# Four-layer cross-attention on one core: projections on column tiles, transposes on row tiles, four score banks

## The chip, the cores and the metric

The kernel runs on one core of one Trainium2 chip. What is measured is the device time of one execution in microseconds (us). A core has a matrix engine (TensorE, "PE" in the profile, its weight loads "PEld"), VectorE (DVE), ScalarE (ACT), GpSimd (POOL) and SyncE (SP, here only the issuer of transfers). TensorE writes into PSUM, which has eight banks here, each of 128 partitions by 512 f32 columns; other engines copy from there to SBUF.

TensorE's array can work whole (128 rows by 128 columns), or divided into tiles: two row tiles of 64 rows, four of 32, two column tiles of 64 columns, or four of 32. Row tiles take operands that are short in the contracted dimension, column tiles take stationary operands with few columns, and several tiles work side by side. Which of these divisions is set is called a mode here.

## The reference

Sixteen batches of queries `x` (100 x 256) pass through four layers of cross-attention with the same context (361 x 256), all in f32. Cut to what matters:

```python
def attention(q, k, v):                       # 16 heads
    return softmax(q @ k.T * scale) @ v

# L0: heads of 16; layer norm of query and context, biases, then a feed-forward block 256 -> 1024 -> 256
x = x + attention(ln(x) @ wq + bq, ln(ctx) @ wk + bk, ln(ctx) @ wv + bv) @ wo + bo
x = x + gelu(ln(x) @ w1 + b1) @ w2 + b2
# L1: heads of 64; RMS norm of the query, plain context
x = x + attention(rms(x) @ wq, ctx @ wk, ctx @ wv) @ wo
# L2: heads of 64; rotary positions on q and k, a mask, layer norm at the end
x = ln(x + attention(rope(x @ Wq), rope(ctx @ Wk), ctx @ Wv, mask) @ Wo) * gamma + beta
# L3: heads of 16; layer norm of query and context, biases
x = x + attention(ln(x) @ Wq + bq, ln(ctx) @ Wk + bk, ln(ctx) @ Wv + bv) @ Wo + bo
```

## The kernel before, in words

All weights are loaded once into SBUF ("slabs") and stay there. A batch is written as a list of pieces of work; each piece is a function that issues a few instructions of one engine, with the buffers it reads, writes and takes. `Plan.add` records it, `Plan.order` sorts all pieces of all sixteen batches into one fixed order by simulating the engines with costs written into the kernel (`on_pe`, `on_dve`, `on_act`, `on_pool`), and the instructions are then issued in that order. So the order on each engine is fixed when the program is built, and pieces of neighbouring batches stand between each other; `plan.order(2.5e4)` sets by how much an older batch goes first.

The planner knows TensorE's modes. Each piece for TensorE has one, `MODE_SWITCH` is the cost that the planner sets for a change of mode, and `KEEP_MODE` a bias toward staying in the mode. There are five: `full` (whole array), `row64`, `row16` (row tiles of 32 rows), `col64`, `col16` (column tiles of 32 columns). For the planner's own count a piece with no mode is a mode of its own.

Which work runs in which mode before:

- `full`: transposes of the context (`keys_T`, L630), once as it is and once normalized; transposes of the queries (`queries_T`, L595), five per batch; keys projections (`project_T`, L618, 361 columns); values projections (L1025 with 512 columns in the layers with heads of 64, L935 with 256 in the others); output projections (`project_out`, L857, 256 columns).
- `col64`: query projections and the first feed-forward product (`project_narrow`, L610, 100 columns); values products of heads of 64 (`weighted`, L814).
- `col16`: values products of heads of 16 (L814), on four column tiles.
- `row64` and `row16`: scores (L703) of heads of 64 and of heads of 16, which stand in strips of 32 rows.
- `row64`: transposes of the probabilities (`transposed`, L782). The rows 0 to 63 and 64 to 99 go to a row tile and a PSUM bank each.

The attention goes in units of four heads. For a unit TensorE writes four score banks; VectorE takes the maximum of each (L753), ScalarE the exponential with its sum (L756), VectorE the reciprocal of the sums (L728), GpSimd multiplies (L735). TensorE transposes the probabilities, VectorE or ScalarE copies them out as `pT` (L545 or L543), and TensorE multiplies them with the values. The helper `copied` (L543, L545) lets the planner choose between ScalarE and VectorE for each copy.

All products and scores share the eight PSUM banks. A second resource, `ps_sc`, has `SCORE_BANKS` = 5 shares; a score bank holds a share until its exponential is done, so that scores can't fill all of PSUM.

The normalized queries `z` (L579) come from statistics on VectorE (L557) and a power on GpSimd (L567), and `queries_T` transposes them.

Of the kernel before, what the change touches and what calls it, by code (L numbers as in the profile page):

```python
# [17 lines left out]
P = 128  # L18
B, S, E = 16, 100, 256
SK = 361  # L20
H = 16
NKC = 3
KC = (128, 128, SK - 256)
SKP = NKC * P
BIG = 3.0e38
SCORE_BANKS = 5

# [39 lines left out]
class Work:  # L67
    __slots__ = (
        "engines", "fn", "bufs", "takes", "next", "then", "n_after", "ready", "tail", "batch",
        "mode", "index", "start", "end", "engine",  # L70
    )
# [24 lines left out]
class Plan:  # L96

    MODE_SWITCH = {"full": 190, "row64": 170, "row16": 170, "col64": 145, "col16": 145, None: 190}

# [19 lines left out]
    def add(self, engines, fn, reads=(), writes=(), takes=(), mode=None, begun=()):  # L119


        w = Work()
        w.engines, w.fn, w.mode, w.batch = engines, fn, mode, self.batch
        w.index = len(self.work)
# [33 lines left out]
    def order(self, lag):  # L158
# [10 lines left out]
        while left:  # L169
# [3 lines left out]
            for w in ready:  # L173
# [24 lines left out]
                for e, occ, lat in w.engines:  # L198
                    s = max(t, free_at[e])
                    if e == "PE" and w.mode != mode:  # L200
                        lat = lat + self.MODE_SWITCH[w.mode]
                    if cost is None or s + lat < cost - 1:
                        engine, cost, start = e, s + lat, s
                late = start
                if engine == "PE" and w.mode != mode and run < self.RUN:
                    late += self.KEEP_MODE
# [5 lines left out]
            if e == "PE":  # L212
                run = run + occ if w.mode == mode else occ
                if w.mode != mode:
                    occ += self.MODE_SWITCH[w.mode]
                mode = w.mode
            free_at[e] = start + occ
            w.start, w.end, w.engine = start, end, e
            for b in w.takes:
                slots = self.free[b.cls]  # L220
                slots.sort()
                _, i = slots.pop(0)
                b.slot, b.ap = i, self.slots[b.cls][i]
                if b.cls in turn:
                    turn[b.cls] += 1
# [22 lines left out]
def tile_xattn_layers(  # L248
# [18 lines left out]
    def slots_of(name, n, shape, dtype=F32, pool=const):  # L267
# [9 lines left out]
        "ctxr": slots_of("ctxr", 1, [P, NKC, E]),  # L277
        "cT": slots_of("cT", 2, [P, 2, SK]),
        "zT": slots_of("zT", 2, [P, 2, SK]),
        "rot": slots_of("rot", 1, [P, 2, SK]),  # L280
# [308 lines left out]
    def queries_T(src, p, name):  # L589

        t, ps = plan.buf(f"xT{p}", name), plan.buf("ps", f"{name}_ps")

        def fn(_):
            for c in range(2):
                nc.tensor.transpose(  # L595
                    ps.ap[:, c * S : (c + 1) * S], src.ap[:, c * P : (c + 1) * P], ident[:S, :S]
                )

        plan.add(on_pe((S, 2)), fn, reads=[src], writes=[ps], takes=[t], mode="full")
        copied(  # L600
            lambda: t.ap.rearrange("p c s -> p (c s)"), lambda: ps.ap[:, : 2 * S], 2 * S, [ps], [t]
        )
        return t

    def project_narrow(ps, wt, m, rhs, n):

        for c in range(2):
            for t in range(2):
                m0 = m * P + t * 64
                nc.tensor.matmul(  # L610
                    ps[t * 64 : (t + 1) * 64, :n], lhsT=wt[:, c, m0 : m0 + 64], rhs=rhs[:, c, :n],
                    start=(c == 0), stop=(c == 1), tile_position=(0, t * 64),
                )

    def project_T(ps, wt, m, rhs, n):

        for c in range(2):
            nc.tensor.matmul(  # L618
                ps[:, :n], lhsT=wt[:, c, m * P : (m + 1) * P], rhs=rhs[:, c, :n],
                start=(c == 0), stop=(c == 1),  # L620
            )

    def keys_T(ct, cls, b):
        t = plan.buf(cls, f"{cls}_{b}")
        for c in range(2):
            ps = plan.buf("ps", f"{cls}_ps_{b}_{c}")

            def fn(_, c=c, ps=ps):
                for j, n in enumerate(KC):
                    nc.tensor.transpose(  # L630
                        ps.ap[:, j * P : j * P + n], ct.ap[:n, j, c * P : (c + 1) * P],
                        ident[:n, :n],
                    )

            plan.add(on_pe((P, 3)), fn, reads=[ct], writes=[ps], takes=[t], mode="full")
            copied(
                lambda c=c: t.ap[:, c, :], lambda ps=ps: ps.ap[:, :SK], SK, [ps], [t]
            )
        return t
# [31 lines left out]
    class Attention:  # L671
# [17 lines left out]
        def unit(self, i):  # L689
# [9 lines left out]
            def scores(_):  # L699
# [11 lines left out]
                on_pe((half, 4 * len(groups))), scores, reads=[self.q, *keys],  # L711
                writes=[*banks.values(), *shares.values()], mode=f"row{hd}",
            )
# [84 lines left out]
        def weighted(self, i, groups, pTs):  # L798
# [4 lines left out]
            def fn(_):  # L803
# [19 lines left out]
                writes=[ps],  # L823
                mode=f"col{hd}",
            )
# [24 lines left out]
    def project_out(oT, nch, wname, resid, p, name):  # L850

        ps, t = plan.buf("ps", f"{name}_ps"), plan.buf(f"x{p}", name)
        wt = w[wname]

        def fn(_):
            for c in range(nch):
                nc.tensor.matmul(  # L857
                    ps.ap[:S, :E], lhsT=oT.ap[:, c, :], rhs=wt[:, c, :], start=(c == 0),
                    stop=(c == nch - 1),
                )  # L860

        def add(_):
            nc.vector.tensor_tensor(t.ap, ps.ap[:S, :E], resid.ap, ALU.add)

        plan.add(
            on_pe((E, 2 * nch)), fn, reads=[oT, slab_of[wname]], writes=[ps], takes=[t], mode="full"
        )
        plan.add(on_dve(E), add, reads=[ps, resid], writes=[t])
        return t


    def small_heads_layer(L, b, xt, zT, names, fq, fk):
# [5 lines left out]
        def keys(m):  # L878
            ps = plan.buf("ps", f"L{L}_k_ps_{b}_{m}")

            def fn(_):
                project_T(ps.ap, w[wk], m, zT.ap, SK)

            def biased(eng):
# [9 lines left out]
            plan.add(  # L894
                on_pe((SK, 4)), fn, reads=[zT, weight(wk)], writes=[ps], takes=[kb[m]], mode="full"
            )
# [14 lines left out]

        def queries(_, ps=ps):
            for m in range(2):
                project_narrow(ps.ap[:, m * S :], w[wq], m, qn.ap, S)

        plan.add(
            on_pe((S, 8)), queries, reads=[qn, weight(wq)], writes=[ps], takes=[qT], mode="col64"
        )
# [11 lines left out]
        for j, n in enumerate(KC):  # L930
            ps = plan.buf("ps", f"L{L}_v_ps_{b}_{j}")

            def values(_, j=j, n=n, ps=ps):
                for c in range(2):
                    nc.tensor.matmul(  # L935
                        ps.ap[:n, :E], lhsT=zT.ap[:, c, j * P : j * P + n], rhs=w[wv][:, c, :],
                        start=(c == 0), stop=(c == 1),
                    )

            plan.add(  # L940
                on_pe((E, 4)), values, reads=[zT, weight(wv)], writes=[ps], takes=[v], mode="full"
            )
# [26 lines left out]
    def large_heads_layer(L, b, xt, xT, cT, names, rot, cap):  # L969
# [4 lines left out]
        for u in range(2):  # L974
            ps = plan.buf("ps", f"L{L}_q_ps_{b}_{u}")

            def queries(_, u=u, ps=ps):
                for m in range(4):
                    project_narrow(ps.ap[:, m * S :], w[wq], 4 * u + m, xT.ap, S)

            def dst(a, u=u):
# [3 lines left out]
                on_pe((S, 16)), queries, reads=[xT, weight(wq)], writes=[ps], takes=[qT],  # L985
                mode="col64",
            )
# [11 lines left out]
        def keys(m):  # L999
            ps, kt = plan.buf("ps", f"L{L}_k_ps_{b}_{m}"), plan.buf(f"kT{p}", f"L{L}_k_{b}_{m}")  # L1000
            kb[m] = kt

            def fn(_):
                project_T(ps.ap, w[wk], m, cT.ap, SK)

            plan.add(
                on_pe((SK, 4)), fn, reads=[cT, weight(wk), *([rot] if rot else [])], writes=[ps],
                takes=[kt], mode="full",
            )
# [8 lines left out]
        def values(half):  # L1018
            v = vb[half] = plan.buf(f"v{p}", f"L{L}_v_{b}_{half}")
            for j, n in enumerate(KC):  # L1020
                ps = plan.buf("ps", f"L{L}_v_ps_{b}_{half}_{j}")

                def fn(_, j=j, n=n, ps=ps):
                    for c in range(2):
                        nc.tensor.matmul(  # L1025
                            ps.ap[:n, :], lhsT=cT.ap[:, c, j * P : j * P + n],
                            rhs=w[wv][:, c, half * 512 : (half + 1) * 512],
                            start=(c == 0), stop=(c == 1),
                        )

                plan.add(
                    on_pe((512, 4)), fn, reads=[cT, weight(wv)], writes=[ps], takes=[v], mode="full"
                )
                copied(
                    lambda j=j, n=n: v.ap[:n, j, :], lambda n=n, ps=ps: ps.ap[:n, :], 512, [ps], [v]
                )
# [20 lines left out]
    def feed_forward(b, xt):  # L1057
# [9 lines left out]

        def hidden(_):
            for f in range(8):
                project_narrow(pss[f // 4].ap[:, f % 4 * S :], w[w1], f, yT.ap, S)  # L1070

        plan.add(
            on_pe((S, 32)), hidden, reads=[yT, weight(w1)], writes=pss, takes=[hT], mode="col64"
        )

# [88 lines left out]
    with tc.manual_schedule():  # L1164
        for work in plan.order(2.5e4):
            if work.fn is not None:
                work.fn(work.engine)

# [48 lines left out]
```

## Time and profile before

| | |
|---|---|
| Runs | 2083.6, 2086.1, 2088.1 us; median 2086.1 |
| The profiled execution | 2088.5 us, of which the profile's span is 2086.4 us |
| Granted TensorE clock, mean | 0.988 |
| TensorE matmul records and instructions of weights | 23,737 each |
| VectorE, ScalarE, GpSimd busy in the span | 68%, 51%, 46% |
| Copies of `pT` on VectorE (L545) | 667, 265.7 us in all |
| Transfers | 27.37 MB, most of it in the first 50 us |

A share of busy time is the time in which at least one instruction of the engine is under way. Matmuls overlap one another, and the ends of their records are modelled, so for TensorE the time from one start to the next says more than a duration. An f32 matmul leaves two records, a transpose one. A row such as `128*64 128x100` is a stationary operand of 128 rows by 64 columns, and a moving operand of 128 rows by 100 columns. Rows of the timeline merge neighbours of one line.

### The profile page before, as it was taken

The page shows a single profiled execution, that of the slowest core. Times are in us where ns is not written, and L with a number is a line of the kernel's source. Part 1 is how long each engine was busy: PE and PEld are TensorE (multiplying, and loading weights), DVE is VectorE, ACT ScalarE, POOL GpSimd, SP SyncE. Part 2 cuts the span into 40 slices and gives each one's busy share as a digit, 9 for nine tenths or more (in the row PEclk, how much of TensorE's full clock was granted, in tenths as well). Part 3 has the DMA queues.
Part 4 walks back from the last instruction along what each step waited for, and adds up shares of the span by engine and source line. Part 5 has one row for each costly group of instructions (what it writes and reads, how often), then busy time and mean ns, then how long its engine had stood idle before and what let it go on. Part 6 is the DMA issues. An engine that isn't in the chain of part 4 may idle for free.

```text
span 2086.4 us, 59681 instructions
## 1 busy us (share of the span) xinstructions
PE 2038.3 (98%) x23737; PEld 1432.2 (69%) x23737; DVE 1409.7 (68%) x4035; ACT 1056.2 (51%) x3190; POOL 955.4 (46%) x1521
## 2 busy tenths in 40 slices
PE   8999999999999999999999999999999999999997
PEld 6667667676776766767676676767667666676765
DVE  4556766767577675776767667676776767767674
ACT  3545445545455454554555555454554545545543
POOL 3244635436254452644526354352544526445362
PEclk9999999999999999999999999999999999999996
DMA  7000000000000000000000000000000000000000
GB/s 282 2 2 12 4 10 4 4 12 4 10 4 4 11 4 12 2 12 4 4 12 4 10 4 4 12 4 10 4 4 12 4 12 4 10 4 4 2 4 3
DMA packets 14430, 27.37 MB, mean 13 GB/s; under 512 B 3346, under 2 KB 12360, under 8 KB 12616
## 3 DMA queue, kind: packets, MB, share of 16 engines
q1 hardware_dynamic: 14152, 23.56, 3.5%
q8 instruction: 187, 3.06, 0.6%
q14 instruction: 91, 0.75, 0.1%
HBM read 21.92 MB, written 1.64 MB: 11 GB/s over the span
## 4 chain that ended last, share of the span: by engine, by line
PE 91%; DVE 5%; ACT 1%; issue 1%; POOL 1%; DMA 1%; SPq 0%; ACTq 0%; DVEq 0%; POOLq 0%
PE ps L618 19%; PE ps L1025 16%; PE ps L703 12%; PE ps L814 11%; PE ps L857 10%; PE ps L782 10%; PE ps L610 6%; PE ps L935 4%; ACT pT L543 1%; PE ps L595 1%; PE ps L630 1%; DVE two L753 1%; DVE mv L557 1%; POOL mv L567 1%; PE ps L441 1%
## 5 line engine op out<-in xcount | busy, mean ns | idle before, releaser
L735 POOL TENSOR_SCALAR prob<-prob,two 100x361 f32<-100x361 f32 x1024 | 569.6, 574 | 559.7 <-DVE two L728 510.6
L756 ACT ACTIVATE prob<-ps,two 100x361 f32<-100x361 f32 x1024 | 564.3, 565 | 128.3 <-DVE two L753 97.4
L753 DVE TENSOR_REDUCE two<-ps 100x1 f32<-100x361 f32 x1024 | 475.9, 523 | 191.9 <-PE ps L703 191.9
L1025 PE MATMUL ps<-slab,cT 128*128 128x512 f32 (+1 forms) x768 | 373.2, 609 | 0.0
L618 PE MATMUL ps<-cT,slab 128*128 128x361 f32 x1024 | 353.7, 483 | 0.5 <-ACT pT L543 0.5
L545 DVE COPY pT<-ps 128x216 f32<-128x216 f32 (+1 forms) x667 | 265.7, 429 | 113.9 <-PE ps L782 103.4
L703 PE MATMUL ps<-kT,qT 32*100 32x181 f32 (+3 forms) x4096 | 303.2, 330 | 0.6 <-DVE qT L923 0.6
L782 PEld LDWEIGHTS ps<-ident,prob 36*128 36x128 f32 (+1 forms) x6144 | 223.7, 140 | 99.4 <-POOL prob L735 41.5
L703 PEld LDWEIGHTS ps<-kT,qT 32*100 32x100 f32 (+1 forms) x4096 | 228.6, 165 | 92.2 <-issue 42.1
L543 ACT COPY pT<-ps 128x384 f32<-128x384 f32 (+1 forms) x357 | 153.1, 461 | 230.1 <-PE ps L782 178.8
L782 PE MATMUL ps<-ident,prob 64*128 64x64 f32 (+1 forms) x6144 | 256.6, 228 | 2.8 <-POOL prob L735 2.0
L618 PEld LDWEIGHTS ps<-cT,slab 128*128 128x128 f32 x1024 | 184.5, 191 | 95.2 <-issue 3.7
L1025 PEld LDWEIGHTS ps<-slab,cT 128*128 128x128 f32 (+1 forms) x768 | 129.3, 183 | 119.8 <-issue 102.4
L756 ACT ACTIVATION_READ_ACCUMULATOR prob<-ps,two 100x1 f32 x1024 | 210.4, 205 | 0.0
L610 PEld LDWEIGHTS ps<-xT,slab 128*64 128x64 f32 x3584 | 157.1, 138 | 41.4 <-ACT prob L756 17.5
L567 POOL TENSOR_TENSOR mv<-mv,neg_half 128x1 f32<-128x1 f32 (+1 forms) x96 | 57.4, 604 | 258.9 <-DVE mv L564 254.4
L610 PE MATMUL ps<-xT,slab 128*64 128x100 f32 x3584 | 172.9, 252 | 0.9 <-ACT xT L543 0.9
L656 POOL TENSOR_TENSOR sw<-sw,rot 128x361 f32<-128x361 f32 x128 | 105.1, 822 | 148.7 <-DVE sw L652 146.2
L543 ACT COPY v<-ps 128x512 f32<-128x512 f32 (+1 forms) x159 | 93.2, 586 | 152.1 <-PE ps L1025 151.1
L814 PE MATMUL ps<-pT,v 128*64 128x100 f32 (+1 forms) x3072 | 152.7, 253 | 5.0 <-ACT pT L543 4.3
L857 PE MATMUL ps<-slab,oT 128*100 128x256 f32 x640 | 152.7, 386 | 0.0
L814 PEld LDWEIGHTS ps<-pT,v 128*64 128x64 f32 (+1 forms) x3072 | 135.9, 137 | 19.2 <-ACT pT L543 6.6
(85 smaller groups left out, 2060.5 us busy)
## 6 DMA issues: line engine op xcount, KB each, us to landing
slab<-slabs_dram SPq DMA_DIRECT2D x12, 1024.0 KB
ctxr<-ctx_dram SPq DMA_DIRECT2D x16, 256.0 KB
ctxr<-ctx_dram SPq DMA_DIRECT2D x16, 105.0 KB
x<-x_dram SPq DMA_DIRECT2D x16, 100.0 KB
out_dram<-x SPq DMA_DIRECT2D x16, 100.0 KB
mask<-mask_dram SPq DMA_DIRECT2D x16, 45.1 KB
rows<-rowvecs_dram SPq DMA_DIRECT2D x1, 640.0 KB
cst<-consts_dram SPq DMA_DIRECT2D x1, 362.0 KB
```

What stands on the lines that cost most here:

```text
L543: nc.scalar.copy(dst(), src())
L545: nc.vector.tensor_copy(dst(), src())
L610: nc.tensor.matmul(ps[t * 64 : (t + 1) * 64, :n], lhsT=wt[:, c, m0 : m0 + 64], rhs=rhs[:, c, :n], start=(c == 0), stop=(c == 1), tile_posi ...
L618: nc.tensor.matmul(ps[:, :n], lhsT=wt[:, c, m * P : (m + 1) * P], rhs=rhs[:, c, :n], start=(c == 0), stop=(c == 1),)
L703: nc.tensor.matmul(banks[h].ap[:S, k0:k1], lhsT=self.q_of(h), rhs=self.k_of(h)[:, k0:k1], start=(k0 == 0), stop=(k1 == SK), skip_group_che ...
L735: nc.gpsimd.tensor_scalar(p.ap[:S, :SK], p.ap[:S, :SK], rsum.ap[:S, j : j + 1], 1.0, ALU.mult, ALU.mult,)
L753: nc.vector.tensor_reduce(neg_max.ap[:S, 0:1], s(), AX.X, ALU.max, negate=True)
L756: nc.scalar.activation(prob.ap[:S, :SK], s(), AF.Exp, bias=neg_max.ap[:S, 0:1], accum_out=sums.ap[:S, j : j + 1],)
L782: nc.tensor.transpose(tp(t)[:, j, c, :], prob.ap[q0:q1, c * P : (c + 1) * P], ident[q0:q1, q0:q1],)
L814: nc.tensor.matmul(ps.ap[t * w0 : (t + 1) * w0, cols], lhsT=lhsT, rhs=pTs[h][0].ap[:n, pTs[h][1], c, :], start=(c == 0), stop=(c == NKC - ...
L857: nc.tensor.matmul(ps.ap[:S, :E], lhsT=oT.ap[:, c, :], rhs=wt[:, c, :], start=(c == 0), stop=(c == nch - 1),)
L1025: nc.tensor.matmul(ps.ap[:n, :], lhsT=cT.ap[:, c, j * P : j * P + n], rhs=w[wv][:, c, half * 512 : (half + 1) * 512], start=(c == 0), stop ...
```

## The change

All work of `full` mode but the one-time set-up of the weights moves to a divided array.

- A new helper `on_columns` splits a product along the columns of its stationary operand, in widths of 64 or 32, one matmul for each column tile. `project_T` uses it and replaces `project_narrow` too; values and output projections call it directly. The last context chunk of 105 rows becomes 64 + 41 or 32 + 32 + 32 + 9, and 100 queries become 64 + 36 or 32 + 32 + 32 + 4.
- Projections take either width: `mode=ANY_COLUMNS`. The planner uses the one that is set, and the first, `col64`, where neither is. The function gets the chosen mode as its argument (`work.fn(work.mode)`).
- `queries_T` and `keys_T` transpose in halves of 64 rows on two row tiles, each into a bank of its own, as `transposed` did before. A query tile is then copied out in two copies of 128 and 72 columns rather than in one of 200. A context tile is one piece of twelve transposes with two banks and three copies of 384, 256 and 82 columns; before, it was two pieces of three transposes, a bank and a copy of 361 columns each. The tiles `cT` and `zT` grow from 361 to 384 columns per half.
- `row16` and `col16` are renamed `row32` and `col32`, which they were in fact; `MODE_SWITCH` has new values.
- `SCORE_BANKS` goes from 5 to 4, and the lag between batches from 2.5e4 to 3e4.

```diff
-SCORE_BANKS = 5
+SCORE_BANKS = 4
...
-    MODE_SWITCH = {"full": 190, "row64": 170, "row16": 170, "col64": 145, "col16": 145, None: 190}
+    MODE_SWITCH = {"row64": 160, "row32": 175, "col64": 145, "col32": 130, None: 190}
...
+        w.modes = mode if isinstance(mode, tuple) else (mode,)
...
-                if engine == "PE" and w.mode != mode and run < self.RUN:
+                if engine == "PE" and mode not in w.modes and run < self.RUN:
                     late += self.KEEP_MODE
...
+                run = run + occ if mode in w.modes else occ
+                if mode not in w.modes:
+                    mode = w.modes[0]
+                    occ += self.MODE_SWITCH[mode]
+                w.mode = mode
...
     def queries_T(src, p, name):
...
+        banks = [plan.buf("ps", f"{name}_ps{i}") for i in range(2)]
+        parts = ((0, 64), (64, S))
...
             for c in range(2):
-                nc.tensor.transpose(
-                    ps.ap[:, c * S : (c + 1) * S], src.ap[:, c * P : (c + 1) * P], ident[:S, :S]
-                )
-
-        plan.add(on_pe((S, 2)), fn, reads=[src], writes=[ps], takes=[t], mode="full")
+                for i, (q0, q1) in enumerate(parts):
+                    nc.tensor.transpose(
+                        tp(i)[:, c, :], src.ap[q0:q1, c * P : (c + 1) * P], ident[q0:q1, q0:q1]
+                    )
+
+        plan.add(
+            on_pe((64, 2), least=55), fn, reads=[src], writes=banks, takes=[t], mode="row64"
+        )
...
+    def on_columns(mode, out_f, lhsT, rhs, start, stop):
+
+        width = int(mode[3:])
+        n = lhsT.shape[1]
+        for t in range(0, n, width):
+            t1 = min(t + width, n)
+            nc.tensor.matmul(
+                out_f(t, t1), lhsT=lhsT[:, t:t1], rhs=rhs, start=start, stop=stop,
+                tile_position=(0, t),
+            )
+
+    def project_T(mode, ps, wt, m, rhs, n):
+
+        for c in range(2):
+            on_columns(
+                mode, lambda t, t1: ps[t:t1, :n], wt[:, c, m * P : (m + 1) * P], rhs[:, c, :n],
+                c == 0, c == 1,
+            )
+
+    ANY_COLUMNS = ("col64", "col32")
+    HALVES = ((0, 64), (64, P))
...
     def keys_T(ct, cls, b):
...
+            for j, n in enumerate(KC):
+                for c in range(2):
+                    for i, (r0, r1) in enumerate(HALVES):
+                        r1 = min(r1, n)
+                        nc.tensor.transpose(
+                            tp(i)[:, c, j, : r1 - r0], ct.ap[r0:r1, j, c * P : (c + 1) * P],
+                            ident[r0:r1, r0:r1],
+                        )
...
+        copied(lambda: dst(0, 0, NKC), lambda: tp(0), 2 * NKC * 64, [banks[0]], [t])
+        copied(lambda: dst(1, 0, 2), lambda: tp(1)[:, :, 0:2, :], 4 * 64, [banks[1]], [t])
         copied(
+            lambda: t.ap[:, :, 2 * P + 64 : SK], lambda: tp(1)[:, :, 2, :last], 2 * last,
+            [banks[1]], [t],
+        )
...
-        def fn(_):
+        def fn(mode):
             for c in range(nch):
-                nc.tensor.matmul(
-                    ps.ap[:S, :E], lhsT=oT.ap[:, c, :], rhs=wt[:, c, :], start=(c == 0),
-                    stop=(c == nch - 1),
+                on_columns(
+                    mode, lambda t0, t1: ps.ap[t0:t1, :E], oT.ap[:, c, :], wt[:, c, :], c == 0,
+                    c == nch - 1,
                 )
...
-            on_pe((E, 2 * nch)), fn, reads=[oT, slab_of[wname]], writes=[ps], takes=[t], mode="full"
+            on_pe((E, 2 * nch)), fn, reads=[oT, slab_of[wname]], writes=[ps], takes=[t],
+            mode=ANY_COLUMNS,
...
-        for work in plan.order(2.5e4):
+        for work in plan.order(3e4):
             if work.fn is not None:
-                work.fn(work.engine)
+                work.fn(work.mode)
```

The keys and values projections and the query projections change in the same way as the output projection shown.

## The prediction

> **What bounds the kernel now.** I read the page's engine totals first, then the chain of waits, then TensorE's waits, then TensorE's timeline inside one batch.
>
> ```profile
> PE 2038.3 (98%) x23737; PEld 1432.2 (69%) x23737; DVE 1409.7 (68%) x4035; ACT 1056.2 (51%) x3190; POOL 955.4 (46%) x1521
> PE   8999999999999999999999999999999999999997
> PE 91%; DVE 5%; ACT 1%; issue 1%; POOL 1%; DMA 1%; SPq 0%; ACTq 0%; DVEq 0%; POOLq 0%
> ```
>
> TensorE is busy 98% of the span and is 91% of the chain that ended last; VectorE, the next, has 677 us idle. So the time is what TensorE has to do, plus the little that it waits. Its waits:
>
> ```profile
> PE ps L595 <- DVE z L579: 18.3, 15, 5.3
> PE ps L814 <- ACT pT L543: 10.5, 47, 0.3
> ```
>
> The columns are total us, times, longest us. All TensorE waits together are 44 us, and these two are most of it: a transpose of normalized queries that waits for VectorE, and the product with the values that waits for its transposed probabilities.
>
> Busy does not mean streaming. In the timeline (start, duration, engine, line, shapes, number of records), the time from one start to the next, where the rows before and after are in another tiling, is the price of a run of matmuls in one tiling:
>
> ```profile
> 1060.23 2.97 PE L610 MATMUL ps<-xT,slab 128*64 128x100 f32 x64
> 1063.13 1.32 PE L782 MATMUL ps<-ident,prob 64*128 64x64 f32 x36
> 1064.39 1.99 PE L935 MATMUL ps<-slab,zT 128*128 128x256 f32 x8
> ...
> 1085.51 0.91 PE L610 MATMUL ps<-xT,slab 128*64 128x100 f32 x16
> 1086.35 1.48 PE L703 MATMUL ps<-kT,qT 64*100 64x181 f32 x16
> ...
> 1094.07 0.58 PE L782 MATMUL ps<-ident,prob 64*128 64x64 f32 x12
> 1094.59 2.70 PE L618 MATMUL ps<-cT,slab 128*128 128x361 f32 x8
> 1097.21 1.48 PE L703 MATMUL ps<-kT,qT 64*100 64x181 f32 x16
> ...
> 1107.39 3.70 PE L857 MATMUL ps<-slab,oT 128*100 128x256 f32 x16
> 1111.02 0.87 PE L703 MATMUL ps<-kT,qT 32*100 32x181 f32 x16
> 1111.82 0.39 PE L595 MATMUL ps<-ident,x 100*128 100x100 f32 x2
> ...
> 1118.10 1.98 PE L1025 MATMUL ps<-slab,cT 128*128 128x512 f32 x4
> 1120.01 1.32 PE L782 MATMUL ps<-ident,prob 64*128 64x64 f32 x36
> ...
> 1123.98 1.24 PE L814 MATMUL ps<-pT,vs 128*32 128x100 f32 x48
> 1125.16 0.58 PE L782 MATMUL ps<-ident,prob 64*128 64x64 f32 x12
> ```
>
> Each f32 matmul leaves two records, a transpose one. Full array: L1025 takes 1120.01 - 1118.10 = 1.91 us for 4 x 512 columns, L857 3.63 us for 16 x 256. The difference, 1.72 us for 2048 columns, is 0.84 ns a column, and 1.91 - 2048 x 0.84 ns leaves 0.19 us that belongs to the run and not to its columns. L618 confirms it: 8 x 361 x 0.84 + 0.19 = 2.62, and it took 2.62. Column tiles of 64: 64 records took 2.90 us and 16 took 0.84, so 0.0429 us a record, 0.0858 for two tiles side by side, and 0.153 us for the run. Column tiles of 32: 48 records in 1.18 us; at half of 0.0429 each they are 1.03, the run 0.15. Transposes on two row tiles: 36 in 1.26 us, 12 in 0.52, so 0.0308 each, and 0.15 a run. Row tiles of 32: 0.80 us for 16 records, of which four strips together stream 4 x 181 x 0.84 = 0.61, and 0.19 is the run's.
>
> The reader is to see two things. A column costs the same on the full array and on a pair of column tiles (100 columns: 0.084 against 0.086 us), so tiling a wide projection gains no streaming. And every run has 0.15 to 0.19 us on top. That, times the number of runs, is what can go.
>
> **What the Trainium skill says.** "TensorEngine Tiling (Array Packing)", Key Properties: "Mode switching requires drain: Changing tiling mode (not just tile) drains the TensorE". The trace agrees, and prices it at the 0.15 to 0.19 us above. The same page, Restrictions: column tiling can't be had together with the transpose mode for f32 input; that is why transposes go to row tiles, and the 6144 of L782 show those at 0.0308 us. The same page, Gotcha 1: two row tiles can't write one PSUM bank at the same time; hence two banks for each transpose step, so more banks held at once. "TensorE: Matmul & The Clock Gate", Part 3, gives 2.38x for three column tiles at 512 columns; that is one pack with its latency, not a stream. The trace shows streams of column tiles at 100 columns only, where they overlap fully.
>
> **The change part by part.**
>
> 1. *Runs.* In the order of the built programs I counted stretches of consecutive matmuls of one tile size. Before: 385 full, 164 column-64, 87 column-32, 325 row-64, 127 row-32, 1088 in all. After: 5, 326, 105, 373 and 127, 936 in all. At the prices above the first are 385 x 0.19 + 164 x 0.153 + 87 x 0.15 + 325 x 0.15 + 127 x 0.19 = 73.2 + 25.1 + 13.1 + 48.8 + 24.1 = 184.3 us, the second 1.0 + 49.9 + 15.8 + 56.0 + 24.1 = 146.8. That is -37.5 us, all on TensorE and so on the path. It has two sources: 152 fewer runs (projections now stand in one run with queries, with values products and with each other), and the cheaper head of a column run (0.153 against 0.19), as 64 columns of weights are loaded in the open rather than 128.
>
> 2. *Streaming of the projections.* Equal by the prices above: 0. The tails (64 + 41 for the last context chunk, 64 + 36 for 100 queries) last as long as the wider tile of a pair, as the full matmul did. More weight loads are issued (29,665 records in place of 23,737), but each lies beside the matmul ahead of it: a 64-column load is 137 ns by the PEld rows, and 86 ns of streaming is enough already in L610, where nothing but the head shows.
>
> 3. *Transposes.* Context: six full ones per tile, (4 x 128 + 2 x 105) x 0.84 ns = 0.61 us, become 12 on row tiles at 0.0308, 0.37 us. 32 of these: -7.7 us. I take 64+64 rows at the price of the 64+36 pairs; if the second tile's longer stream shows, 0.1 us each and 3 us come back. Queries: 2 x 100 x 0.84 = 0.168 us become 4 x 0.0308 = 0.123; 80 of these, -3.6 us. Together -11.3.
>
> 4. *Copies.* A context tile takes three copies rather than two, a query tile two rather than one: 112 more on VectorE and ScalarE. By the fixed share of a copy (ACT 332 ns for 200 columns, 586 for 512, so about 0.17 us) this is some 19 us over two engines which have 677 and 1030 us idle. Cost on the path 0, unless the extra copy ends last ahead of a projection; at most 80 x 0.17 = 14 us, unlikely whole because the planner sets other work there.
>
> 5. *Waits.* The order of the changed program puts transposes straight before a column-32 values product 64 times, 37 before. The row of L814 gives 10.5 us over 47 waits, 0.22 us each, for the copy that has to come between; 27 more are +6 us. Nothing on TensorE's queue can pass it.
>
> 6. *Four score banks and the larger lag.* Scores of the next unit need all four earlier shares free rather than three of five; the work kept behind is whatever follows on TensorE. Priced along the order, the median way from a score group's end to its transposes shrinks from 7.9 to 7.3 us, the lowest tenth from 4.95 to 4.7: about the cover that the exponentials had before. The last batch, which runs alone, ends 50 us of TensorE work after the other rather than 46. I charge +2 us for both; bounds: -13 us (the waits for z in the steady part go, as they are a matter of order) to +25 us (0.1 us for each of 256 units).
>
> Sum: -37.5 - 11.3 + 6 + 2 = -41 us. The profiled execution has a span of 2086.4 us and a time of 2088.5; the median of the runs is 2086.1. The sum taken from the median gives 2045 us.
>
> **The rivals.**
>
> *Waits take half.* With fewer runs TensorE asks sooner for every copy and exponential, banks are held in pairs, and scores hold four. For it: 7.3 against 7.9 us of cover, and the 64 tight neighbours. Against: VectorE rises only to about 70%. With +25 us from point 6: 2070 us.
>
> *Waits go too.* The wait of about 1 us for z, once in most batches (13 us in the steady part), is covered by the new order: 2045 - 13 = 2032.
>
> *Column tiles don't hold the rate on long streams (slower).* The widest evidence for column tiles is 100 columns; now 361, 512 and 256 run on them, and each tile reads its own copy of the moving rows. The full-array streams that move are 1280 records x 361 + 768 x 512 + 1280 x 256 columns, 1.18 million x 0.84 ns = 993 us. A loss of 4.1% there eats the 41 us, 5% makes it slower. At 10% the time is 2045 + 99 = 2144 us. Against it: 100-column matmuls run back to back for 2.9 us in L610 with the same sum of reads and writes, at 2% over the full array's price.
>
> **How the numbers follow.** As forecast, 2032 to 2058: 0.55. Waits take half, 2058 to 2078: 0.18. Waits go too, 2018 to 2032: 0.20. Slower streams: 0.05; about even: 0.02. A difference of 0.2%, 4 us, is about what a measurement of this kernel can tell from none. Faster 0.93, same 0.02, slower 0.05. The range 2022 to 2068 holds the forecast's cases and the near half of both neighbours, about 0.8.
>
> **What would show it.** No matmul on the full array but for the set-up; the projections' column-64 rows at 0.84 to 0.86 ns a column for a pair; a run of column tiles with 0.15 us on top; L656's twelve transposes at about 0.37 us. Wrong: start-to-start of a 512-column pair well above 0.43 us (the slower rival), or TensorE's wait rows growing from 44 us to 70 or more (the first rival).

## The result and the profile after

The changed kernel takes 2067.7 us in the median (2065.1 to 2068.2); the kernel before, run beside it, 2086.8 us. The ratio is 0.9908, 95% interval 0.9891 to 0.9925: 19 us less, where the forecast was 41. The profiled execution has a span of 2066.0 us.

The engine totals and the chain of waits of the changed kernel:

```profile
PE 1993.2 (96%) x29665; PEld 1294.4 (63%) x29665; DVE 1375.9 (67%) x4058; ACT 1075.6 (52%) x3277; POOL 965.4 (47%) x1523
PE 85%; DVE 6%; POOL 4%; ACT 3%; issue 2%; DMA 0%; SPq 0%; DVEq 0%; ACTq 0%; POOLq 0%
```

TensorE is busy 45.1 us less than before (2038.3 to 1993.2), but the span fell by only 20.4 us: its idle time rose from 48.1 to 72.8 us. The share of TensorE in the chain fell from 91% to 85%; VectorE, GpSimd and ScalarE took its place. So the work went as forecast and something else came. TensorE's waits (engine and line, who was waited for, total us, times, longest):

```profile
PE ps L851 <- ACT pT L547: 17.3, 68, 1.3
PE ps L627 <- ACT pT L547: 10.2, 46, 0.2
PE ps L819 <- POOL prob L772: 8.1, 12, 1.6
PE ps L627 <- DVE kT L696: 6.6, 13, 0.5
PE ps L413 <- DMA crow<-colvecs_dram: 6.3, 1, 6.3
PE ps L607 <- DVE z L583: 5.3, 1, 5.3
```

L851 is the values product, L627 every projection, L819 the transposes of the probabilities, L607 those of the queries. The wait for z, 13 us in the steady part before (110 to 1975 us), is gone but for one at the end, where the last batch runs alone. All these rows sum to 67.4 us, before to 44.1. Nearly new are 10.2 us in which a *projection* waits for the copy of `pT`; before, the like was one small row of the keys projection:

```profile
PE ps L618 <- ACT pT L543: 0.5, 2, 0.3
```

A projection reads a context or a query tile and a weight; it never reads `pT`. The only thing that such a copy gives it is the PSUM bank which the copy empties. The timeline shows one such wait, and the prices of the changed work beside it:

```profile
972.47 0.96 PE L819 MATMUL ps<-ident,prob 64*128 64x64 f32 x24
973.67 1.94 PE L627 MATMUL ps<-slab,cT 128*64 128x512 f32 x8 [0.24 <-ACT pT L547]
975.54 0.96 PE L819 MATMUL ps<-ident,prob 64*128 64x64 f32 x24
...
991.01 0.58 PE L656 MATMUL ps<-ident,ctxr 64*128 64x64 f32 x12
991.41 1.45 PE L740 MATMUL ps<-kT,qT 64*100 64x181 f32 x16
...
1010.40 2.65 PE L627 MATMUL ps<-cT,slab 128*64 128x361 f32 x16 [0.24 <-ACT pT L547]
1012.98 0.87 PE L740 MATMUL ps<-kT,qT 32*100 32x181 f32 x16
```

The values projection at 973.67 us starts after 24 transposes of probabilities and 0.24 us of idle. From there to the next start it takes 1.87 us for 4 pairs of 512 columns: 4 x 512 x 0.84 ns is 1.72, and 0.15 is the run's. At 1010.40 us, 8 pairs of 361 columns take 2.58 us = 2.43 + 0.15. Twelve transposes of the context take 0.40 us, where I had put 0.37. So in these two runs of long streams two column tiles hold the rate of the full array, to 0.01 us.

For the experiments I made the prices of the prediction sharper in one way: a robust fit over all runs of the trace of before, with a price for each column, matmul, transpose and run of one tiling, applied to the order of any kernel. This sum is what "priced TensorE work" means in the expectations. It is 2001 us for the kernel before and 1946 us for the changed one, 55 less (by hand I had 49). What the span has over it, the *rest*, is waits, start and end, time at a lowered clock, and what the prices miss: 85 us before, 120 us after. As the prices were fitted to the trace of before, the rest of the others may be some us too large; the idle time, which the profile shows, rose by 25 us where the rest rose by 35. The expectations speak of "waits" of 74 and 107 us; that is the rest without the 11 to 13 us around the first and last matmul.

### The profile page after: what moved, and what is told of

Same layout as the page of the kernel before. It is cut to its first block, busy times and chain, and to the rows that moved or that the text cites. A ratio compares the mean times of both kernels' runs of the same rounds, so it can differ in the third digit from the quotient of the medians.

```text
span 2066.0 us, 71693 instructions
## 1 busy us (share of the span) xinstructions
PE 1993.2 (96%) x29665; PEld 1294.4 (63%) x29665; DVE 1375.9 (67%) x4058; ACT 1075.6 (52%) x3277; POOL 965.4 (47%) x1523
## 4 chain that ended last, share of the span: by engine, by line
PE 85%; DVE 6%; POOL 4%; ACT 3%; issue 2%; DMA 0%; SPq 0%; DVEq 0%; ACTq 0%; POOLq 0%
PE ps L627 53%; PE ps L740 12%; PE ps L851 11%; PE ps L819 8%; ACT pT L547 3%; DVE two L790 1%; POOL prob L772 1%; POOL mv L571 1%; DVE ps L787 1%; DVE mv L561 1%; DVE ctxr L1145 1%; POOL kT L701 1%; PE ps L607 1%; PE ps L445 1%; DVE sw L689 1%
## 5 line engine op out<-in xcount | busy, mean ns | idle before, releaser
L627 PE MATMUL ps<-slab,cT 128*32 128x512 f32 (+3 forms) x2232 | 364.9, 596 | 3.7 <-ACT pT L547 3.7
L627 PE MATMUL ps<-cT,slab 128*64 128x361 f32 (+1 forms) x2360 | 351.0, 472 | 13.2 <-DVE kT L696 6.6
L819 PEld LDWEIGHTS ps<-ident,prob 64*128 64x128 f32 (+1 forms) x6144 | 227.4, 140 | 105.8 <-issue 58.7
L549 DVE COPY pT<-ps 128x216 f32<-128x216 f32 (+1 forms) x586 | 230.4, 418 | 93.4 <-PE ps L819 88.0
L819 PE MATMUL ps<-ident,prob 64*128 64x64 f32 (+1 forms) x6144 | 261.9, 229 | 10.4 <-POOL prob L772 8.1
L627 PEld LDWEIGHTS ps<-cT,slab 128*64 128x64 f32 (+1 forms) x2360 | 132.6, 129 | 130.9 <-issue 95.4
L627 PEld LDWEIGHTS ps<-slab,cT 128*32 128x32 f32 (+3 forms) x2232 | 94.8, 117 | 144.9 <-issue 134.1
L627 PE MATMUL ps<-xT,slab 128*64 128x100 f32 (+1 forms) x4576 | 172.6, 251 | 1.8 <-issue 1.4
L627 PEld LDWEIGHTS ps<-xT,slab 128*64 128x64 f32 (+1 forms) x4576 | 162.1, 126 | 19.3 <-issue 11.3
L851 PE MATMUL ps<-pT,v 128*64 128x100 f32 (+1 forms) x3072 | 157.1, 252 | 9.4 <-ACT pT L547 9.4
L851 PEld LDWEIGHTS ps<-pT,v 128*64 128x64 f32 (+1 forms) x3072 | 140.9, 137 | 35.1 <-issue 16.7
L627 PE MATMUL ps<-slab,oT 128*32 128x256 f32 (+2 forms) x1528 | 153.6, 386 | 0.0
L765 DVE RECIPROCAL two<-two 100x2 f32<-100x2 f32 x512 | 81.6, 160 | 91.3 <-ACT prob L793 86.2
## 6 DMA issues: line engine op xcount, KB each, us to landing
mask<-mask_dram SPq DMA_DIRECT2D x16, 45.1 KB
```

The source lines that it names most:

```text
L549: nc.vector.tensor_copy(dst(), src())
L627: nc.tensor.matmul(out_f(t, t1), lhsT=lhsT[:, t:t1], rhs=rhs, start=start, stop=stop, tile_position=(0, t),)
L765: nc.vector.reciprocal(rsum.ap[:S], sums.ap[:S])
L819: nc.tensor.transpose(tp(t)[:, j, c, :], prob.ap[q0:q1, c * P : (c + 1) * P], ident[q0:q1, q0:q1],)
L851: nc.tensor.matmul(ps.ap[t * w0 : (t + 1) * w0, cols], lhsT=lhsT, rhs=pTs[h][0].ap[:n, pTs[h][1], c, :], start=(c == 0), stop=(c == NKC - ...
```

## The experiments

All were compared with runs of the kernel before on the same chip. "Idle" is the span less TensorE's busy time on the page; runs are stretches of one tiling, counted in the order of the built program.

| kernel | median us | ratio, 95% interval | runs | priced work | rest | idle |
|---|---|---|---|---|---|---|
| before | 2086 to 2087 | 1 | 1088 | 2001 | 85 | 48 |
| changed | 2067.7 | 0.9908 (0.9891, 0.9925) | 936 | 1946 | 120 | 73 |
| settings alone | 2129.7 | 1.0209 (1.0193, 1.0224) | 1045 | 1992 | 137 | 80 |
| changed, old settings | 2063.1 | 0.9888 (0.9873, 0.9903) | 1008 | 1957 | 105 | 62 |
| changed, full transposes | 2093.9 | 1.0046 (1.0030, 1.0063) | 955 | 1969 | 123 | 71 |
| row transposes alone | 2116.6 | 1.0152 (1.0137, 1.0167) | 1126 | 1991 | 123 | 69 |
| changed, width 64 alone | 2096.9 | 1.0055 (1.0040, 1.0070) | 1096 | 1970 | 125 | 77 |
| changed, three banks | 2052.0 | 0.9835 (0.9819, 0.9852) | 927 | 1945 | 107 | 56 |
| before, three banks | 2130.8 | 1.0219 (1.0203, 1.0234) | 1042 | 2003 | 126 | 72 |
| changed, short copies | 2042.0 | 0.9781 (0.9767, 0.9796) | 936 | 1946 | 95 | 47 |
| before, lag 3e4 | 2130.8 | 1.0211 (1.0196, 1.0226) | 1137 | 2008 | 121 | 78 |
| changed, lag 3.1e4 | 2129.2 | 1.0204 (1.0187, 1.0221) | 967 | 1951 | 175 | 108 |
| three banks, 5 shares, lag 3.2e4 | 2029.4 | 0.9736 (0.9717, 0.9755) | 892 | 1940 | 88 | 47 |

### The two settings, alone and taken back

```diff
-SCORE_BANKS = 5
+SCORE_BANKS = 4
...
-        for work in plan.order(2.5e4):
+        for work in plan.order(3e4):
```

> The kernel before with only the two planner settings of the change (four score shares, lag 3e4). TensorE's instructions at the prices of the kernel before sum to 1992 us (before: 2001), some 12 us lie around them, and the waits decide. If the added waits of the changed kernel come from the settings: waits of 107 us as there, so about 2110 us. If they come from its work (faster TensorE, banks held in pairs by the transposes): waits of 74 us as before, so about 2078 us.

The other kernel is the changed one with the same two lines reversed.

> The changed kernel with the old settings (five score shares, lag 2.5e4). Priced TensorE work 1957 us (changed kernel: 1946). If the settings cause the added waits: 74 us of waits, about 2043 us. If not: 107 us, about 2076 us.

The settings alone make the kernel before 44 us slower, with less TensorE work and a rest of 137 us: more waits than either expectation. The changed kernel with the old settings takes 2063 us, between its two expectations, a rest of 105 us. Neither theory fits both: the settings are not the whole cause of the changed kernel's waits, since of its 35 us more rest 20 stay without them, but a new order brought far more waits to the old pieces. With the settings alone the largest rows are still those of the kernel before, for z (18.3 us there) and for `pT` (10.5), and the rise is spread over many small ones; the third line is the largest of these:

```profile
PE ps L595 <- DVE z L579: 23.8, 15, 5.4
PE ps L814 <- ACT pT L543: 9.6, 45, 0.2
PE ps L610 <- ACT xT L543: 6.7, 16, 0.4
```

### The parts of the change

The changed kernel with `queries_T` and `keys_T` of the kernel before (and a price for "full" in `MODE_SWITCH`):

> The changed kernel with the transposes of context and queries on the full array again, in one bank each. Priced TensorE work 1969 us. If holding two banks at once for these transposes causes the added waits: back to 74 us, about 2055 us. If the row transposes are a plain gain and the waits stay: 107 us, about 2088 us.

The kernel before with the `queries_T` and `keys_T` of the change:

> The kernel before with the transposes of context and queries on row tiles and two banks, projections on the full array, old settings. Priced TensorE work 1991 us (before: 2001). If the waits stay at 74 us: about 2077 us. If the pairs of banks cost as many waits as the changed kernel has (107 us): about 2110 us.

The changed kernel with one width:

```diff
-    ANY_COLUMNS = ("col64", "col32")
+    ANY_COLUMNS = "col64"
```

> The changed kernel with projections bound to column tiles of 64, not to whichever width is set. The order has 1096 runs of one tiling where the changed kernel has 936; priced TensorE work 1970 us against 1946. If a run costs what the kernel before shows: 24 us more work, with waits of 107 us about 2090 us. If the choice of width is worth nothing because waits fill the place of the drains: about 2066 us.

None of the three gains. Column tiles without row transposes take 2094 us, row transposes without column tiles 2117 us, both by the expectation that has the larger waits. Holding two banks for context and queries can't be the cause by itself, as the first of them doesn't do it and waits as much. Of the three, the third is the cleanest on price: without the choice of width the order has 160 runs more and 24 us more priced work, and the kernel is 29 us slower with a rest that differs by 5. With 1096 runs it has even 8 more than the kernel before. So in these orders the choice of width, which I hadn't costed by itself, carries the whole drop in the number of runs, and 24 of the 55 us.

### Waits for a bank: three in place of four

A unit transposes the probabilities of two pairs of heads, each into two banks: 384 columns of rows 0 to 63, and 216 of rows 64 to 99. In this kernel the two smaller parts share a bank (432 columns); each pair keeps its copies.

```diff
-            banks = [plan.buf("ps", f"{name}_tp{t}") for t in range(2)]
-            pT = plan.buf("pT", f"{name}_pT")
+            firsts = [plan.buf("ps", f"{name}_tpa{u}") for u in range(2)]
+            rest = plan.buf("ps", f"{name}_tpb")
+            pTs = [plan.buf("pT", f"{name}_{u}_pT") for u in range(2)]
...
+                    writes=[firsts[u], rest], takes=pTs, mode="row64",
```

> The changed kernel where a unit's two probability transposes share the bank of rows 64 to 99, so that a unit holds three banks for its transposes and not four. Priced TensorE work 1945 us, as in the changed kernel. If TensorE's added waits are for a free PSUM bank (all eight held by four scores and four transposes): the 32 us of waits right behind probability transposes go, about 2034 us, and waits of L851 and L627 for the copy of pT nearly vanish. If they are waits for the data of the copy: no change, 2060 to 2070 us.

It takes 2052 us, 16 less than the changed kernel, with the same priced work. The two rows that it was made against nearly vanish; the values product is L860 here. Other waits rise: the one for z is back with 12.8 us.

```profile
PE ps L607 <- DVE z L583: 12.8, 12, 5.3
PE ps L823 <- POOL prob L770: 8.1, 16, 1.8
PE ps L627 <- DVE kT L696: 6.6, 13, 0.5
...
PE ps L860 <- ACT pT L547: 3.7, 6, 0.9
...
PE ps L627 <- ACT pT L547: 0.5, 2, 0.2
```

Following each PSUM bank through the traces, from its first matmul to the last read, says the same; this can be done because the planner fixes which bank each piece gets. In the steady part (110 to 1950 us) the changed kernel has 103 waits behind probability transposes in which all eight banks were held, four by scores and four by transposes, and the bank of the next product had only just been emptied: about 31 us, counted from start to start over the usual time. With three banks for a unit, 3 such waits are left, 0.9 us. The kernel before has 44, 13 us.

The same count over the whole span, by the idle time of the wait rows, gives 35 us of waits for a bank in the changed kernel and 11 in the kernel before. All its other waits are 32 and 33 us. So the rise in its wait rows, 23 us, is all waits for a bank. The values product does read `pT`, but in 66 of the 68 waits of L851 the copies that it reads had ended at least 2.5 us before, and what ended some 0.05 us before its start was the copy out of the bank that it writes. The same holds for all 47 waits of L814 in the kernel before.

The three-bank kernel has an order of its own, so its time doesn't prove the cause for the changed kernel's order. The next experiment keeps that order on every engine, and shortens what holds the bank. It leaves out two thirds of the transposed probabilities, so it serves for timing alone.

```diff
             copied(
-                lambda q0=q0, q1=q1: pT.ap[:, :, :, q0:q1], lambda t=t: tp(t),
+                lambda q0=q0, q1=q1: pT.ap[:, :, 0:1, q0:q1], lambda t=t: tp(t)[:, :, 0:1, :],
                 2 * NKC * (q1 - q0), [banks[t]], [pT],
             )
```

> The changed kernel in its own order on every engine; only the copies of pT out of PSUM carry the first of three context chunks (the other two thirds are left at zero), so that a transpose bank comes free some 0.2 us sooner, and the values products read the same tiles. TensorE's work is unchanged at 1946 us. If the waits behind probability transposes are for a bank that such a copy still holds: the 27 us of waits of L851 and L627 on pT go, about 2040 us. If they are for something else (probabilities, statistics): 2060 us or more.

It takes 2042 us; against the changed kernel the ratio falls by 0.0127, about 26 us. Its waits, where L853 is the values product, L629 the projections and L821 the transposes:

```profile
PE ps L821 <- POOL prob L774: 8.6, 13, 1.6
PE ps L629 <- DVE kT L698: 6.7, 13, 0.5
...
PE ps L853 <- DVE pT L551: 3.4, 3, 1.3
...
PE ps L853 <- ACT pT L549: 1.5, 3, 0.7
```

The projections' wait for `pT` is gone from the list, and the values products' is down from 17.3 us to 1.5, with 3.4 on copies of VectorE beside it, while the waits on GpSimd and on `kT` are what they were. So the 27 us of waits on these copies are shown, in the changed kernel's own order, to hang on how long a copy takes. Shorter copies also bring `pT` sooner and leave ScalarE and VectorE 79 and 97 us less to do, so for the values products this run alone doesn't part the bank from the data. The projections, which read no `pT`, and the count of banks above do.

### How much of the waits belongs to the order

> The kernel before, its own pieces and five shares, with a lag of 3e4: only the order differs. Priced TensorE work 2008 us (before: 2001). If the low waits of the kernel before belong to its pieces: 74 us, about 2094 us. If they belong to the one order, and another order of the same pieces waits as the other re-ordered kernels did (92 to 127 us): 2112 to 2147 us.

> The changed kernel with a lag of 3.1e4 in place of 3e4. Priced TensorE work 1951 us (changed kernel: 1946). If the waits of the changed kernel belong to its pieces: 107 us, about 2071 us. If a small step of the lag redraws the order and the waits with it: 20 us or more from that.

The edits are the number in `plan.order` alone. The kernel before with a lag of 3e4 is 43 us slower, 7 of them priced work and 36 more rest. The changed kernel with 3.1e4 in place of 3e4 is 61 us slower than the changed kernel; 5 us are work, 55 us rest. Idle time is 35 us of the 55. It has one wait of 3.1 us 14 times, which the changed kernel has once:

```profile
PE ps L627 <- ACT prob L793: 43.0, 14, 3.1
PE ps L656 <- DVE ctxr L1145: 11.8, 13, 1.0
```

This wait, too, is for a bank, one that held scores until their exponential ended 0.14 us before; what the product reads had been done for 4 us. And it costs more than itself. At or just after each of the 14 the trace shows a stretch of 3.4 us in which the granted clock is 0.5, and the product that waited is slower. Here is one, and below it the same product in the changed kernel, without the wait:

```profile
1069.70 5.08 PE L627 MATMUL ps<-slab,qT 128*64 128x256 f32 x32 [3.07 <-ACT prob L793]
1074.71 1.48 PE L740 MATMUL ps<-kT,qT 64*100 64x181 f32 x16
...
1042.20 3.62 PE L627 MATMUL ps<-slab,qT 128*64 128x256 f32 x32
1045.76 1.48 PE L740 MATMUL ps<-kT,qT 64*100 64x181 f32 x16
```

From start to start it takes 5.01 us in place of 3.56. The mean granted clock is 0.979 over a span of 2125.6 us, and 0.988 over 2066.0 us in the changed kernel. I estimate from these that 45 in place of 25 us at full clock are missing, 20 us more, which is the part of the 55 that is not idle time.

Both expectations of a redrawn order hold, that of pieces with their own fixed waits falls. The waits of an order are a matter of that order, in the kernel before as in the changed one: with a step of one number the rest of the same pieces moves by 36 or 55 us, more than the change's gain.

### Three banks in the kernel before, and a faster version

> The kernel before with three banks for a unit's probability transposes rather than four. Priced TensorE work 2003 us (before: 2001). Its waits for a free bank are 13 us: if sharing takes those away and adds none, 2003 + 61 + 12 = 2076 us; if the order it leads to brings others, 2088 us or more.

2131 us. The waits for a bank fall, from 11 to 6 us by the count above, but the order brings other waits, for z (22.3 us) and for probabilities on GpSimd (16.2 us), and a lower mean clock, 0.982. So freeing a bank was no gain by itself.

> The changed kernel with three banks for a unit's transposes, five score shares and a lag of 3.2e4. The order has 892 runs, priced TensorE work 1940 us. With the waits of the three-bank kernel (95 us): 2048 us. If the fifth share can be held without filling the eight banks, waits of 74 us: 2026 us.

2029.4 us, 0.9736 of the kernel before: faster than both kernels, 38 us below the changed one. It combines the three banks with the fifth score share and a lag of 3.2e4; what each of the two settings adds to the three banks alone (2052 us) was not run. The settings were chosen among some twenty lags by the gaps that the planner's own costs left on TensorE; they are a good draw and no rule. Its page and its waits:

```profile
PE 1980.8 (98%) x29825; PEld 1289.7 (64%) x29825; DVE 1396.2 (69%) x4014; ACT 1096.0 (54%) x3321; POOL 965.3 (48%) x1523
PE ps L656 <- DVE ctxr L1154: 11.6, 14, 1.0
PE ps L607 <- DVE z L583: 8.8, 15, 5.3
PE ps L823 <- ACT pT L547: 3.8, 15, 0.3
PE ps L860 <- ACT pT L547: 2.1, 3, 0.9
```

TensorE is back at 98%, with an idle time of 47 us as before, on 61 us less priced work. Of what bounded the changed kernel, the waits on `pT`, 6 us are left.

## Why the prediction was right and wrong

**Steps 1 to 3, TensorE's own work: right.** The forecast was -37.5 us for runs, 0 for streams, -11.3 for transposes, -49 together. That lies between the fit, -55 for the same counts, and the page, 45 us less busy; of the page's figure a little is missing, because a wait behind a matmul hides partly in its record, which runs on to its modelled end. Where the runs went I had only in part: it is the choice of width, not column tiles as such, that makes them fewer. Streams of 512 and 361 columns in column tiles cost what I took from 100 columns, and the slower rival has nothing left. No run here writes one bank from two row tiles at once, or transposes on column tiles; for these two limits the prediction has a page's word alone.

**Step 4, the copies: nothing on the path, as forecast.** TensorE's rows for the copies of queries and context are 0.5 us (`xT`) and 0.7 us (`zT`). ScalarE's busy time is 19 us up and VectorE's 34 down, as the planner moved copies of `pT` from VectorE to ScalarE; VectorE is at 67%, ScalarE at 52%.

**Step 5, waits behind transposes: the term that failed, in its kind and size.** I counted 27 more values products straight behind transposes and charged 6 us for the copy "that has to come between", taking the wait for one on data. L851's row did rise by 6.8 us (10.5 to 17.3). But the wait is for a bank, and so was the row of L814 from which I read it: in all of its 47 waits the data had been there for 2.5 us or more. Such a wait falls on whatever comes next, a projection as well. The 46 waits of L627 for `pT`, 10.2 us, were not in my sum, because I looked only for instructions that read `pT`. The wait for `kT`, 6.6 us behind context transposes, is of the same kind: in these 13 waits, too, all eight banks were held, two of them by the context's transposes.

**Step 6, settings and order: under-sized.** I charged +2 us, with bounds of -13 and +25, as if the waits of before were a property of the kernel to which the change adds some. With step 5 that made 8 us of added waits. TensorE's wait rows grew by 23 us, its idle time by 25, and the rest by 35 (85 to 120). The step of reasoning that failed is to take the waits of the one order that was profiled as the base of the new one. Of the eleven kernels made for the experiments none has a rest below 88 us, and seven have 121 to 175 us. The kernel before, at 85, is the lowest. By idle time two of the eleven, short copies and the last version, come to its 48 us (47 each).

The rival "waits take half", 2070 us with a chance of 0.18, is what happened, and its sign, wait rows of 70 us, all but came (67.4). Its mechanism of banks in demand was the right one; the numbers that I weighed for and against it (the median cover of 7.3 against 7.9 us, VectorE at 70%) say nothing about a moment in which all eight banks are full. What can't be divided cleanly is the added waits between pieces and order. That they are waits for a bank is shown, and with short copies the same order is 26 us faster. But the old pieces have 19 us of such waits with a lag of 3e4, and 28 with both settings, in place of 11. Why the planner found an order with so few of them for the kernel before, and not here, I haven't tried to settle beyond showing that such luck didn't survive a change of the lag.

## What to carry to other kernels

On an engine at 98%, price a change of tiling by counting runs of one mode and the time from start to start; here that sum, 49 us, came within 6 us of a fit and of the fall in busy time. Waits can't be carried over in the same way where a planner lays a new order: treat those of the old order as a favourable draw, expect more, and judge a change by more than one setting. And when the instruction that waits doesn't read what it waits for, count the banks.

## What the runs showed that I had not expected

The size of the order's share: a lag of 3.1e4 in place of 3e4, with the same pieces of work, cost 61 us or 3%, a third of it by the clock, which was halved for 3.4 us at each of 14 waits of 3.1 us. And column tiles, as forecast, held the full array's rate on long streams, on uneven tiles too: an output projection of 64 + 36 queries, 32 records of 256 columns, took 3.60 us from its start (968.06 us in the timeline) to the next run's, 16 x 256 x 0.84 ns + 0.15.
